# Two graph-attention layers in one timetable: further shifts for the places of the steps

## Chip, cores, metric

The kernel runs on one core of a Trainium2 chip. The metric is the device time of one execution in microseconds. The time before is the median of three runs; one further execution was profiled.

## What is computed

Sixteen graphs of 1024 nodes with 256 features pass through two pre-normed layers that share one adjacency matrix. The first layer holds an MLP, an attention without a mask (call it Dense), a second MLP and a masked attention (`a`); the second layer is one masked attention (`b`). Cut to what matters:

```python
def reference(x, adj, w1, b1, w2, b2, W_fc, a_fc, W_hand, a_hand, W_l1, a_l1):
    h = maximum(layernorm(x), 0)
    res = relu(h @ w1 + b1)
    out = elu(gat(res, None, W_fc, a_fc, slope=0.2)) + res      # Dense: every node sees all
    res = relu(out @ w2 + b2)
    x = x + relu(elu(gat(res, adj, W_hand, a_hand, slope=0.2)) + res)   # a
    h = maximum(layernorm(x), 0)
    return x + relu(gat(h, adj, W_l1, a_l1, slope=0.01))                # b
def gat(inp, mask, W, a):
    h = inp @ W
    e = leaky_relu((h @ a[:F])[:, :, None] + (h @ a[F:])[:, None, :])
    return softmax(where(mask, e, -inf), axis=2) @ h            # elu after it inside the first layer
```

## The kernel before

Each graph is one "batch" `b` of eight row tiles of 128 nodes. The softmax weights factor: for `a` and `b` a weight is the larger of two products of a node's number with a neighbour's, times the 0/1 mask. So VectorE makes a tile of weights in one instruction (`weight`, L645: tiles `atta` and `attb`, 128 x 256) from a row that is broadcast over the partitions (`rows`), and TensorE multiplies two such tiles of 128 with a tile of projected features (`product`, L655). A column of numbers becomes a broadcast row by way of DRAM: TensorE turns it (`send_row`, L474), ScalarE copies the 8 x 128 line (L476) and issues its DMA to `row_a`, `row_b` or `row_r` (L477); SyncE, after the line has landed, issues the read that broadcasts it (`row`, L630 for `a` and `b`, L759 for Dense). In the last batches TensorE broadcasts the row itself.

Dense has no mask, so from the second batch on it is not a product of matrices: nodes are ranked (`rank`, VectorE, L786 to L793), scattered in order of rank to DRAM (`scatter`, GpSimd indirect DMA, L800, one for each tile of nodes; it needs that tile's `project(t, 0)`, its `fs` copy at L744 and its rank), read back sorted (`read_sorted`, SyncE, L844, tile `xs`), summed from both ends (`sum_before`, `sum_behind`, tiles `tt` and `xs`), written as tables (`write_table`, L879; `carry`, L896 and L901) and gathered (`gather`, GpSimd, L912: a fine and a coarse one for each tile). `share` and `mean` make the mean, `merge` (L984 to L988) and `merge_end` (L994, and GpSimd's add at L995) turn and add it, `mlp2` (L1002, copy by ScalarE L1005) follows. `Norm` takes statistics (`stats`, L494, `root`, L499 and L500), centers (`center`, L504) and turns tiles on TensorE (`turn`, L514, copy L518); `BlockNorm` moves blocks by DMA instead (`move`, L560). `natural` turns the second MLP's output back (L1016, L1018).

Every one of 6508 steps stands in a list with a time that was written by hand, and a shift is added to it:

```python
    def at(name, lo, hi, steps):
        for i, step in enumerate(steps):
            key = part + name
            moved = SHIFT.get(key, ())
            k = turn[key] = turn.get(key, -1) + 1
            when = lo + (hi - lo) * i / len(steps) + (moved[k] if k < len(moved) else 0.0)
            table.append((when, len(table), step))
```

`part` is "start " ahead of the first period, then "first ", "mid " (batches 1 to 12) and "end " (the last three); `turn` counts the uses of a name inside one period. A missing entry is a shift of nothing. At the end the list is sorted by `when`, and the steps are emitted in that order. On TensorE, VectorE, ScalarE and SyncE the instructions run in that order exactly, and the scheduler is told to keep GpSimd's order too, the scatters free among themselves. Times in the list do nothing but sort: no instruction waits for a clock. A step that stands in a queue waits for its operands and holds up all that stands behind it.

A period is 142 of the list's units for each batch: `masked_first` (attention `a`), `second_norm`, `masked_second` (products of `b`, the last three quarters of them in the next batch's period), `dense_sums`, `early_gathers`, `dense_end` for the next batch and `first_mlp`, `dense_rows`, `dense_begin` for the one after it. In `masked_first` the order of `a` is `masked_first1` (`vectors`: the three exponentials of the factors), `masked_first2` (`send`), `masked_first3` (`row`), `weights a` and `masked_first9` (`product`). PSUM has four buffers named `mm` for products and projections; ScalarE or VectorE must have read one before it is used again. Tiles of weights have eight buffers, broadcast rows two.

Of the kernel before, what the change touches and what calls it, by code (L numbers as in the profile page):

```python
# [30 lines left out]
    "end dense_begin5": (3.85, 3.85,),  # L31
    "end dense_begin6": (0, 0, 0, -3.04, -3.77, -12.93,),
    "end dense_begin7": (5.89,),
    "end dense_end1": (-6.28, -0.87,),
    "end dense_end2": (1.33, -1.87, -0.43, -1.02, 1.01, 1.01, 1.01, 1.01,),
    "end dense_rows1": (-5.54, 0, 0, -5.65, 0, 0, -5.89, -12.08,),
    "end dense_sums10": (-30.04,),
    "end dense_sums12": (6.2,),
    "end dense_sums2": (7.2, 0, 16.96, 0, -1.45, 0, 4.23, 7.81,),
    "end dense_sums3": (-5.9, -5.22,),  # L40
    "end dense_sums4": (-1.96, -1.96, -1.96, -1.96,),
    "end dense_sums6": (5.6,),
    "end dense_sums7": (0, -0.43, -1.68, -1.93, -2.8, -4.51, 0, 2.83,),
    "end dense_sums9": (4.27,),
    "end early_gathers1": (2.05, 8.49,),
    "end early_gathers2": (2.39, 2.39,),
    "end early_gathers3": (0, 0, 0, 13.54,),
    "end early_gathers4": (3.94, 3.94, 3.94, 3.94, 3.94, 3.94, 3.94, 3.94,),
    "end first_mlp1": (-4.68, 0, 0, 5.61,),
    "end first_mlp2": (0, 0, 0, -3.18,),  # L50
    "end masked_first1": (-5.71,),
    "end masked_first10": (0, -1.8, -2.88, -3.79, -1.77, 1.09, -1.61, -2.39,),
    "end masked_first11": (0, 0, 1.72, 0, -1.95, 0, -1.34, -1.8,),
    "end masked_first12": (-2.14, -0.57,),
    "end masked_first13": (1.32, 1.3, 0.19, -1.57, -1.22, 0, -0.9, -0.54,),
    "end masked_first14": (1.17, 2.08, 1.51, 0, 5.36, 0, 2.26,),
    "end masked_first16": (1.34,),
    "end masked_first2": (-5.62,),
    "end masked_first4": (-2.61,),
    "end masked_first5": (-3.63, -2.25, -1.64, -1.44,),  # L60
    "end masked_first7": (-16.12, -7.04, 0, 27.99,),
    "end masked_first8": (-14.41, 0, 0, -12.41,),
    "end masked_first9": (-1.61, -1.61, -1.61, -1.61, -1.61, -1.61, -1.61, -1.61, -3.83, -3.83,
        -3.83, -3.83, -3.83, -3.83, -3.83, -3.83, -1.88, -1.88, -1.88, -1.88, -1.88, -1.88, -1.88,
        -1.88, -4.28, -3.4, -3, -2.75, -2.49, -2.68, -1.93, -2.03, -6.69, -6.37, -6.2, -4.96,
        -5.03, -3.23, -2.35, -1.84,),
    "end masked_second1": (0.66, 0.66, 0.66, 0.66, 0.66, 0.66, -2.34, -2.03, -0.87, -1.67, 0, 0,
        -3.2, -3.01, -2.28, -2.11, -1.88, -1.38, 0, 0, 0, 0, 0, 0, -4.13, -2.16, -1.71, -1.96, 0,
        1.01, -5.79, -3.22, -2.37, 0, 0, 3.34,),
    "end masked_second2": (0, 0, 0, 0, -1.59, 0.14, 1.34, 1.34, 2.34, 1.98, 0, 3.96,),  # L70
    "end masked_second3": (0, -1.37, 1.51, 0, 0, 2.39, 1.49, 3.1,),
    "end masked_second4": (2.68, 5.78, 3.49, 0, 1.55, 1.12, 1.78, 5.03,),
    "end masked_second5": (12.24, 5.75, 8.78, 18.18, 17.51, 10.76,),
    "end masked_second6": (7.07, 9.36,),
    "end merges1": (0, -1.03, -0.3, -2.41, 4.74, 0.64, 1.64,),
    "end merges2": (-0.27, -1.56, -1.28, 3.77, 3.14,),
    "end scatters1": (4.29, -1.28, 0, -3.35, 0, -3.76, 0, -5.98,),
    "end second_mlp1": (1.75, 3.03, 13.57,),
    "end second_mlp2": (-7.98, -7.98, -7.98, -7.98, -7.98, -7.98, -7.98, -7.98,),
    "end second_mlp3": (-6.19,),  # L80
    "end second_norm1": (-2.07, 0, -0.95, -3.91, -2.7, -3.39, -4.37, -5.24,),
    "end second_norm2": (-5.55,),
    "end second_norm3": (-5.42,),
    "end second_norm4": (-3.38,),
    "end second_norm5": (-3.12, -0.71, -6.35, -2.61, -0.69,),
    "end second_norm6": (-1.66,),
    "end turn_at1": (0.72, 5.74, 4.57, 6.67, 0.93, 0.93, 0.93, 0.93,),
    "end turn_at2": (2.47, 2.47, 2.47, 2.47, 0.67, 0.87, 0.71, 0.9,),
    "end weights a": (-4.01, -4.48, -2.31, 0, -2.36, 0, 0, 2.96, -5.53, -0.61, -1.24, 0, -8.38,
        -6.95, 0, 0.62, -1.94, 0, -4.51, -7.54, -1.94, 0, 0, 0, -3.5, -22.43, -2.3, -2.55, -4.46,  # L90
        -0.67, -3.44, -19, -5.33, -5.1, -4.83, -26.42, -2.06, 0, -5.18, -4.76,),
    "end weights b": (-2.94, -1.93, 0, -4.78, -1.01, -0.6, 0, 2.13, -2.64, 0.84, -5.47, 0, 0.22,
        -2.95, -0.53, 1.64, -4.25, -7.92, -4.22, -2.6, -2.98, -9.67, -4.08, 0.95, 1.1, 0, 0, 0,
        -5.56, -0.87, 0, 1.83, -4.94, -2.59, -2.4, -4.98, 0, 2.22, 3.49, 2.79, -2.87, -2.87, -2.87,
        -2.87, -2.87, -2.87, -2.87, -2.87,),
    "first dense_begin2": (1, 4.41,),
    "first dense_begin3": (-1.89,),
    "first dense_begin4": (0, -3.14,),
    "first dense_begin5": (-13.99, -4.89,),
    "first dense_begin6": (-10.16, -24.55, -16.26, -13.59, -20.39, -20.4,),  # L100
    "first dense_begin7": (26.94,),
    "first dense_begin8": (8.17,),
    "first dense_end1": (0, -4.85,),
    "first dense_rows1": (0, 14.27, -1.34, 0, 0, 0, 0, -10.26,),
    "first first_mlp1": (0, 4.41, 24.43,),
    "first first_mlp2": (5.97, 17.04, 15.82,),
    "first first_norm3": (-21.29, -20.06, -15.24, -17.2, -23.42, -19.12, -5.58, -19.77,),
    "first first_norm4": (-1.34,),
    "first first_norm5": (0, -2.84, 6.7, -8.53,),
    "first first_norm6": (16.39, 14.37, 17.56, 0, 0, 8.81, 12.12, 10.28,),  # L110
    "first first_norm7": (27.8, 27.8, 27.8, 27.8,),
    "first first_norm8": (21.34, 21.34, 21.34, 21.34,),
    "first gathers1": (0, 0, 0, 0, 10.07, 13.53, 11.92, 8.19,),
    "first gathers2": (1.94, 0, 0, 7.94, 0, 0, 0, -4.73,),
    "first masked_first1": (-3.19,),
    "first masked_first10": (0, 0, 0, -0.95, 0, 0, -0.98,),
    "first masked_first11": (3.59, 0, 2.07, 0, 3.1, 0, -2.17, 0.49,),
    "first masked_first13": (0, 4.59, 0, 0, 3.21, 0, -3.57, -3.16,),
    "first masked_first14": (2.35, 8.59, 1.68, 0, 2.92, 1.37, -3.45, -4.07,),
    "first masked_first15": (-2.27,),  # L120
    "first masked_first16": (-4.48,),
    "first masked_first4": (-3.2,),
    "first masked_first9": (0, 0, 0, 0, 0, 0, 0, 0, 0, 0, 0, 0, 0, 0, 0, 0, -1.65, -1.65, -1.65,
        -1.65, -1.65, -1.65, -1.65, -1.65,),
    "first masked_second1": (-6.69, -6.69, -6.69, -6.69, -6.69, -6.69, -5.31, -5.31, -5.31, -5.31,
        -5.31, -5.31,),
    "first masked_second2": (-5.39, -5.39, -3.53, -3.53,),
    "first masked_second3": (-5.97, 0, 0, 0, 0, 0, 4.48,),
    "first masked_second4": (7.23, 7.93, 0, 0, 20.56, 0, 15.38,),
    "first masked_second6": (44.24, 33.84,),  # L130
    "first merges1": (0, -0.51, 0, 3.1, 0, 0.67, 0, 1.56,),
    "first merges2": (1.94, 1.94, 1.94, 1.94,),
    "first scatters1": (0, 0, 0, 0, 0, 0, 11.81, 7.33,),
    "first second_mlp1": (0, 0, 7.25,),
    "first second_mlp2": (-6.32, -6.32, -6.32, -6.32, -6.32, -6.32, -6.32, -6.32,),
    "first second_norm1": (1.12, 0.5, 4.9, 2.6, 5.13, 3.86, 3.83, 2.75,),
    "first second_norm2": (2.35,),
    "first second_norm7": (-3.9,),
    "first second_norm8": (10.06, 8.39, 6.47, 15.18,),
    "first start51": (-5.5,),  # L140
    "first turn_at1": (-7.72, -9.85, -6.6, -9.06,),
    "first turn_at2": (-8.2, -6.53, -6.35, -4.27,),
    "first weights a": (0, 0, 0, 0, 0, 0, 0, 0, 0, 0, 0, 0, 0, 0, 0, 0, 0, 0, 0, 0, 0, 1.81, 2.27,
        0, 0, -3.96, -13.89, -7.05, -4.57,),
    "first weights b": (-10.9, -6.04, -9.42, -13.57, -24.74, -13.19, -25.26, -13.17, -9.33, -2.06,
        -2.02, -10.77, -3.64, 0, 0, -19.37, -3.07, -1.96, -1.75, -3.62, -5, -4.1, -5.96, 0, -15.31,
        0, 0, 0, 0, -18.05,),
    "mid dense_begin1": (-4.18,),
    "mid dense_begin3": (-5.24,),
    "mid dense_begin5": (-10.75,),  # L150
    "mid dense_begin6": (0, 0, -21.24, -17.26, -3.32, -3.92,),
# [1683 lines left out]
```

## Time and profile before

| | us |
| --- | --- |
| median of three runs (lowest, highest) | 2287.52 (2285.39, 2288.34) |
| the profiled execution, its own time | 2288.26 |
| its span, first to last instruction | 2286.5 |
| TensorE busy | 2217.3 (97%) |
| VectorE busy | 1626.2 (71%) |
| ScalarE busy | 1263.9 (55%) |
| GpSimd busy | 958.8 (42%) |
| granted TensorE clock | 0.997 |

Busy time is summed for each engine over the span; 1.8 us of the execution lie outside it. A row of a group of instructions gives the line, the engine, out<-in with shapes and count, then busy us and mean ns of one, then the idle time just before them and who ended it. A row of waits gives who waited, for whom, the us in total, the number of times and the longest. A row of the timeline gives start and length in us, the instruction, and in brackets the idle time before it.

### The profile page before, as it was taken

Reading aid. Unit: us, or ns where it says so; the run is one execution under the profiler, and the core shown is the slowest. Engines: PE = TensorE matmul, PEld = TensorE weight load, DVE = VectorE, ACT = ScalarE, POOL = GpSimd, SP = SyncE. Lnnn points to the kernel's source line nnn. Section 1 sums busy time; section 2 is a strip of 40 time slices with the busy share of each in tenths; the row PEclk is TensorE's granted clock in tenths of the full one; section 3 lists DMA queues with packets and bytes.
Section 4 is the critical chain, followed back from the end, with each engine's and each line's share of the span. In section 5 each row is a group of like instructions: output and inputs, shape, how many; then the busy total and the mean of one; then the engine's idle time right before and its main releaser. Section 6 shows DMA issues by size and latency. Waiting matters only on the chain. (4 is left out here: it accounts for less than half of the span.)

```text
span 2286.5 us, 31026 instructions
## 1 busy us (share of the span) xinstructions
PE 2217.3 (97%) x9754; PEld 1721.6 (75%) x9754; DVE 1626.2 (71%) x4535; ACT 1263.9 (55%) x2797; POOL 958.8 (42%) x1212
## 2 busy tenths in 40 slices
PE   8989999999999999999999999999999999999997
PEld 5766677787877868777787877868777787878776
DVE  7667586676867768776676867768776776858755
ACT  5355656557465563746557374564755557365552
POOL 1253325263442635436263442636435263443520
PEclk9999999999999999999999999999999999999999
DMA  4568367574666747567674666747466674655600
GB/s 175 179 175 199 87 183 181 163 204 126 204 134 186 191 145 201 122 188 171 178 191 133 196 134 188 191 149 205 117 202 152 184 194 133 179 117 170 180 21 28
DMA packets 263870, 368.95 MB, mean 161 GB/s; under 512 B 124353, under 2 KB 175881, under 8 KB 259601
## 3 DMA queue, kind: packets, MB, share of 16 engines
q1 hardware_dynamic: 217088, 202.72, 32.0%
q0 software_dynamic: 45952, 163.99, 27.6%
q8 instruction: 80, 1.31, 0.2%
q14 instruction: 94, 0.76, 0.1%
q10 hardware_dynamic: 656, 0.17, 0.0%
HBM read 226.88 MB, written 126.29 MB: 154 GB/s over the span
## 5 line engine op out<-in xcount | busy, mean ns | idle before, releaser
L655 PE MATMUL oa<-hma,atta 128*128 128x258 f32 x2048 | 463.9, 383 | 20.8 <-DVE atta L645 18.2
L655 PE MATMUL ob<-hmb,attb 128*128 128x257 f32 x2048 | 467.0, 381 | 4.1 <-DVE attb L645 4.1
L740 PE MATMUL h<-wfc_sb,resT 128*128 128x257 f32 x2048 | 468.1, 379 | 0.0
L655 PEld LDWEIGHTS oa<-hma,atta 128*128 128x128 f32 x2048 | 383.6, 190 | 90.1 <-issue 27.0
L655 PEld LDWEIGHTS ob<-hmb,attb 128*128 128x128 f32 x2048 | 383.4, 190 | 72.5 <-issue 13.3
L740 PEld LDWEIGHTS h<-wfc_sb,resT 128*128 128x128 f32 x2048 | 379.7, 189 | 71.5 <-issue 19.7
L683 POOL TENSOR_TENSOR posa<-posa,onat 128x256 f32<-128x256 f32 x118 | 107.6, 912 | 485.7 <-ACT posa L671 485.6
L645 DVE SCALAR_TENSOR_TENSOR attb<-rowsb,qwdb,edge 128x256 f32<-128x256 f32 (+1 forms) x536 | 256.3, 497 | 51.6 <-PE ob L655 38.1
L645 DVE SCALAR_TENSOR_TENSOR atta<-rowsa,qwda,edge 128x256 f32<-128x256 f32 (+1 forms) x520 | 249.7, 513 | 58.2 <-DMA rowsa<-row_a 50.5
L995 POOL TENSOR_TENSOR resT<-resT,e 128x512 f32<-128x512 f32 x128 | 164.0, 1283 | 270.5 <-DVE e L994 245.7
L912 POOL DMA_INDIRECT got<-coarse,k x124 | 204.1, 1646 | 112.7 <-DMA got<-fine,k 73.1
L726 PE MATMUL m<-hT,w_sb 128*128 128x512 f32 x512 | 237.5, 598 | 0.6 <-ACT hT L518 0.5
L1002 PE MATMUL m<-resT,w_sb 128*128 128x512 f32 x512 | 230.9, 595 | 2.9 <-POOL resT L995 2.6
L697 ACT ACTIVATE rb<-ob,recb 128x256 f32<-128x256 f32 x128 | 59.0, 474 | 314.5 <-DVE recb L695 302.7
L670 ACT ACTIVATE ea<-oa,reca 128x256 f32<-128x256 f32 x128 | 60.6, 473 | 240.5 <-DVE reca L667 224.1
L912 POOL DMA_INDIRECT got<-fine,k x124 | 129.4, 1043 | 102.8 <-DVE attd L958 38.3
L1002 PEld LDWEIGHTS m<-resT,w_sb 128*128 128x128 f32 x512 | 94.8, 191 | 100.2 <-issue 87.1
L726 PEld LDWEIGHTS m<-hT,w_sb 128*128 128x128 f32 x512 | 94.3, 192 | 86.4 <-issue 77.9
L800 POOL DMA_INDIRECT sorted<-hnat,place x128 | 129.5, 1011 | 41.7 <-issue 23.9
L823 ACT ACTIVATE junk<-r,fs 128x1024 int8<-128x1024 f32 x124 | 142.2, 1147 | 6.4 <-ACT linea L476 4.5
L986 DVE TENSOR_SCALAR e<-hpT 128x512 f32<-128x512 f32 x128 | 86.4, 679 | 80.9 <-PE hpT L984 65.3
L994 DVE SCALAR_TENSOR_TENSOR e<-hpT,e 128x512 f32<-128x512 f32 x128 | 87.9, 687 | 47.7 <-ACT e L988 47.2
(195 smaller groups left out, 3420.7 us busy)
## 6 DMA issues: line engine op xcount, KB each, us to landing
xs<-sorted SPq DMA_DIRECT2D x32, 1028.0 KB
fine<-tt SPq DMA_DIRECT2D x32, 1026.0 KB
fine<-xs SPq DMA_DIRECT2D x32, 1026.0 KB
x<-in_x_dram SPq DMA_DIRECT2D x16, 1024.0 KB
xn<-in_x_dram SPq DMA_DIRECT2D x15, 1024.0 KB
out_dram<-x SPq DMA_DIRECT2D x28, 512.0 KB
hT<-xn SPq DMA_DIRECT2D x416, 32.0 KB
coarse<-carry SPq DMA_DIRECT2D x32, 256.5 KB
```

The lines of the kernel that those rows point to most:

```text
L645: nc.vector.scalar_tensor_tensor(a_t[:, :n * P], self.rows[:, i], self.qwd[:, 1, j:j + 1], edge[:, j, i], op0=OP.max, op1=OP.mult)
L655: nc.tensor.matmul(self.out[t][:, :F + self.ONES], lhsT=self.att[t0, j][:, (t - t0) * P:(t - t0 + 1) * P], rhs=self.hm[:, j, 2:2 + F + sel ...
L683: adder.tensor_add(pos, pos, o_nat[:, t, :])
L726: nc.tensor.matmul(ps, lhsT=w1_sb[:, kc, c * P:(c + 1) * P], rhs=piece(kc, h), start=(kc == 0), stop=(kc == FC - 1))
L740: nc.tensor.matmul(ps[:, :F + 1], lhsT=self.resT[:, kc, t * P:(t + 1) * P], rhs=wfc_sb[:, kc, g, :], start=(kc == 0), stop=(kc == HC - 1))
L800: made = nc.gpsimd.indirect_dma_start(out=sorted_d[self.b % 2], out_offset=bass.IndirectOffsetOnAxis(ap=self.place[:, t:t + 1], axis=0), i ...
L823: nc.scalar.activation(junk, self.r2, AF.Sign, bias=self.fs[:, 0, t:t + 1], accum_out=self.signs[:, t:t + 1])
L912: nc.gpsimd.indirect_dma_start(out=got[u // n][:, u % n, :], out_offset=None, in_=(coarse_d if coarse else fine_d)[self.b % 2][:, :], in_o ...
L986: nc.vector.tensor_scalar_min(e, ps, 0.0)
L994: nc.vector.scalar_tensor_tensor(e, ps, 0.0, e, op0=OP.max, op1=OP.add)
L995: nc.gpsimd.tensor_add(dst, dst, e)
L1002: nc.tensor.matmul(ps, lhsT=w2_sb[:, kc, c * P:(c + 1) * P], rhs=self.resT[:, kc, h * HALF:(h + 1) * HALF], start=(kc == 0), stop=(kc == H ...
```

## The change

The table `SHIFT` is replaced: 197 keys before, 215 after, nearly all values differ. No other line of the program changes, and no instruction is added, removed or resized. The values came from a search over a model of the program in which the lines of the rows, and the reads of them, land later than in the model behind the old values. Cut to the entries that the prediction speaks of (many keys hold one value per step):

```diff
-    "mid masked_first1": (2.17,),
-    "mid masked_first2": (1.67,),
+    "mid masked_first2": (-2.08,),
-    "mid weights a": (-0.95, -1.77, -0.69, -0.29, -1.4, -6.11, 0, 0, -4.55, -7.3, 0, 0, 0, 0, 0, 0,
+    "mid weights a": (-5.61, -5.61, -5.61, -5.61, -5.61, -5.61, -5.61, -5.61, -3.71, -9.93, -3.34,
...
+    "mid dense_begin4": (2.24, 0, -1.8, 0, -9.71,),
-    "mid dense_begin6": (0, 0, -21.24, -17.26, -3.32, -3.92,),
+    "mid dense_begin6": (-11.19, 0, -28.74, -20.88, -19.69, -15.58,),
+    "mid dense_begin7": (-8.63,),
+    "mid dense_sums1": (-47.98,),
-    "mid scatters1": (-1.68, -1.68, -1.68, -1.68, -1.68, -1.68, -1.68, -1.68,),
+    "mid scatters1": (0, 0, -7.81, 0, -16.13,),
-    "mid second_norm9": (12.89,),
+    "mid second_norm9": (-12.33,),
-    "mid masked_second1": (-6.06, -4.38, -4.96, -4.4, -4.02, -4.85, -2.93, -3.71, -0.98, -1.47,
+    "mid masked_second1": (-19.72, -6.34, -5.21, -5.4, -5.04, -4.23, 0, 0, 0, 0, 0, 0, 0, 0, 0, 0,
...
-    "mid masked_second3": (0, 0, 1.76, -0.96, 3.75,),
+    "mid masked_second3": (-1.99, -2.6, 0.2, -1.04, 0, 0, 0, 24.02,),
-    "mid turn_at1": (0, 0, 2.19, -5.82,),
-    "mid turn_at2": (3.05, 3.05, 3.05, 3.05, 4.51, 4.51, 4.51, 4.51,),
+    "mid turn_at1": (2.3, 2.3, 2.3, 2.3, 3.13, 3.13, 3.13, 3.13,),
+    "mid turn_at2": (0, 0, 0, 3.05, 4.36, 4.36, 4.36, 4.36,),
-    "start start27": (11.76, 5.71,),
+    "start start27": (-2.71,),
-    "start gathers2": (8.37, 12.36, 13.46, 9.14,),
+    "start gathers2": (0, 7.74, 0, 4.99,),
```

For batch 5, whose period starts at 682 in the list, this puts `vectors` at 683.00 (685.17 before), `send` at 683.32 (687.07), the first product of `a` at 697.55 (700.00), `project(t, 0)` of the Dense of batch 6 for t = 2, 6 and 7 at 649.81, 649.98 and 656.25 (661.00, 666.35 and 667.91) and its scatters in the order 4, 2, 0, 1, 3, 5, 6, 7 (0 to 7 before).

## The prediction

> **What bounds the kernel now.** I read the page's first part, then TensorE's waits by stage, then the timeline of one period.
>
> ```profile
> span 2286.5 us, 31026 instructions
> PE 2217.3 (97%) x9754; PEld 1721.6 (75%) x9754; DVE 1626.2 (71%) x4535; ACT 1263.9 (55%) x2797; POOL 958.8 (42%) x1212
> ```
>
> TensorE is the bound. Of its 69.2 us without work, 10.8 lie before its first transpose and about 10.6 after its last one (ended near 2275.9); no place in a timetable removes the 2217.3. So all that this change can win is in some 48 us of gaps. Where they are, by TensorE's waits, first in 250 to 1900 us (twelve alike periods of 137 us), then in 0 to 250 us:
>
> ```profile
> PE oa L655 <- DVE atta L645: 17.4, 12, 1.9
> PE pa L592 <- issue: 0.8, 1, 0.8
> ```
>
> ```profile
> PE nt L514 <- DVE hn L504: 14.3, 3, 10.8
> PE hpT L984 <- issue: 4.0, 1, 4.0
> PE m L1002 <- POOL resT L995: 2.6, 2, 2.1
> ```
>
> The middle has one fault, 1.45 us in every period; the start has 10.8 (the first load) and some 15 more; the end (1900 on) has 12 us in pieces of up to 1.2. The fault, by the timeline of the period of batch 5:
>
> ```profile
> 841.33 0.80 SPq L844 DMA_DIRECT2D xs<-sorted  x2
> ...
> 844.66 0.27 ACTq L477 DMA_DIRECT2D row_a<-linea  x1
> ...
> 849.76 0.32 SPq L630 DMA_DIRECT2D rowsa<-row_a  x1
> ...
> 854.19 0.48 DVE L645 SCALAR_TENSOR_TENSOR atta<-rowsa,qwda,edge 128x256 f32<-128x256 f32 x1 [4.58 <-DMA rowsa<-row_a]
> ```
>
> The line of 4 KB is issued at 844.66, and SP gets past its landing 5.1 us later; the read of the rows takes 4.4 more; VectorE has stood 4.58 us. Then TensorE waits for the third atta, since before computes j = 5, 1, 0 in that order and product j = 0 comes first: it starts at 856.28. The same kind of line without big company:
>
> ```profile
> 811.64 0.27 ACTq L477 DMA_DIRECT2D row_r<-line  x1
> ...
> 812.86 0.34 SPq L759 DMA_DIRECT2D r<-row_r  x1
> ```
>
> 1.2 us. So the line of `a` is late because 2 MB of xs, issued 3.3 us ahead of it, are in its way; and xs is issued at 841.33 because of the last scatter:
>
> ```profile
> 828.67 1.11 POOL L800 DMA_INDIRECT sorted<-hnat,place  x1 [0.30 <-issue]
> 832.06 0.19 POOL L744 COPY fs<-hnat 128x1 f32<-128x1 f32 x1 [2.29 <-ACT hnat L742]
> ...
> 838.45 0.97 POOL L800 DMA_INDIRECT sorted<-hnat,place  x1 [0.30 <-issue]
> 841.32 0.53 POOL L859 MEMSET tt<- 128x513 f32 x1 [1.91 <-DMA sorted<-hnat,place]
> ```
>
> GpSimd stood 2.29 us for a projection and then issued scatters back to back every 1.3 us up to 838.45, though the last rank was ready at 834.9.
>
> **What the Trainium skill says.** *DMA: Bandwidth & Descriptors*, "Queues, rings and completion order": SP and ACT own one ring each on the same 16 engines, and an engine drains a whole packet of one ring before it turns to another. The trace agrees: 5.1 us behind xs, 1.2 alone. The same page, "Anatomy of one DMA", puts some 2 us of fixed cost on a DMA, most of it the write's receipt; here the lone line took 1.2, and I use that. *TensorE: Matmul & The Clock Gate*, "Step-by-step": only weight loads are pulled ahead, matmuls stay in order; so a late atta stops all of TensorE, as the 17.4 us show.
>
> **The change, part by part.** A step's time is lo + (hi - lo) i / n + shift; sorting all 6508 steps by it gives each queue's order, before and after. No instruction is added or taken away; what counts is how much of TensorE's work lies between two steps. I price it from back-to-back rows: 28 passes of 258 columns in 6.26 us are 0.22 a pass, 0.87 for a masked product of two tiles or a projection of `a` or `b`, 1.74 for a `project` of Dense or an `mlp1`.
>
> *Rows of `a`, twelve periods.* (i) Scatters: `project(t,0)` for t = 6, 7, 2 move 16.4, 11.7 and 11.2 us earlier in the timetable, rank 4 comes first, and the scatters go 4, 2, 0, 1, 3, 5, 6, 7. None waits then for a projection, and GpSimd (1.3 us a scatter) keeps up with VectorE (about 2 us a rank). The memset of tt, which stood in the queue behind the scatters, goes 48 us earlier. Between the first rank and rank 7 stand 1.3 us of other VectorE work (two weights, `query`), as much as the weight and its wait in before, and the row r is read no later (SP's four moves ahead of it, 16 issues of 0.65 us, fit before its line lands). So rank 7 is ready near 834.5, its scatter goes out at once, and xs is issued near 834.5 + 2.9 = 837.4 (838.45 to 841.33 in before), 4 us earlier. (ii) `vectors` to first product holds 12.1 us of TensorE work after and 13.4 before. On the clock of this period `vectors` begins at 841.4 (841.04 in before, and 0.4 more of TensorE's work is ahead of it); the line is issued 3.3 later, 844.7; the last of xs lands near 837.4 + 7.5 = 844.9; the line by 846.2; rows 4.4 later, 850.6; the first atta, now j = 0, at 851.1. TensorE comes there at 841.4 + 12.1 = 853.5: 2.4 us to spare. If xs does not move, rows land at 854.1, atta at 854.7, and 1.2 of the wait stay. I take the first and leave 0.9 us over twelve periods: **-16.5** (ends -3 and -17.4).
>
> *Waits that come in their place, twelve periods.* `center` 4 to 7 of the second norm now stand behind `finish(6)` of `b` on VectorE. From the end of its product: 0.45 drain, 0.16 reciprocal, four centers at 0.4, `update(6)` between them held by ScalarE's 0.47: the last is ready at 2.8; TensorE has 1.74 (two projections) and three turns of 0.22 before it needs it, 2.4: some 0.4 us. `vectors` of `a` waits for the last projection's copy, behind sign 6 (1.26 us) on ScalarE: 0.15 to 0.2. The copy of `mlp2(1,1)` now stands behind `query`, just on time. Sum 0.6 a period: **+7** (ends 0 and +14). Behind a center that waits there are only centers on VectorE, and the turn and projections on TensorE.
>
> *Start.* `carry` 0 and 1 move 16.6 and 7.9 us of TensorE work earlier, so the coarse gathers (issued 121.91 to 134.25 in before) can go from about 115, and the merges that stood 4.0 + 0.7 us at 144 find their data. The second norm of batch 0 turns some 9 us of TensorE work later, which covers its 3.5. Against it: four allocations of a PSUM buffer with 0 to 0.87 us of work since its last use, where a copy takes 0.9 to 1.4: +2. The 2.6 at 156 stays. Of -6 I take **-4** (ends -8 and +2).
>
> *End.* In batch 14 `vectors` to first product of `b` grows from 3.0 to 5.6 us of work, against 4.8 that it took; in 15 by 0.4 for `a` and `b`. -3 is in sight, but this stretch changes most and I follow it least: **-1.5** (ends -5 and +4).
>
> Other moves (stores, loads of x, the reads of rows `b` 25 us earlier, atts up to 20 us ahead) I cost at nothing: the least work between a weight and its product grows from 0.9 to 2.6 us for `a` and from 1.7 to 4.4 for `b`, and TensorE's work covers them. Without that cover each late weight is 0.5 us. SP's queue: gb's read no longer stands before a move that it could hold up, and the load of x, now ahead of the first table write, delays that by up to 5 us, which has 28 us until its gather.
>
> Sum -16.5 + 7 - 4 - 1.5 = -15. The profiled execution took 2288.26 (span 2286.5 and 1.8 around it), which gives 2273.3; it lies 0.7 over the median of the runs, 2287.52, from which I predict **2272.5**.
>
> **Rivals.** *The line stays behind xs* (r, ranks or scatters no faster; or the plan's order is not the bound of GpSimd): the rows' part gives only the atta order, -3 to -5, new waits +3 to +7, start and end -5: 2282 to 2288, no difference. For it: 1 us of delay in r's row shifts the whole chain. Against: 2.4 us of slack.
>
> *Slower: PSUM buffers held too long.* The first product of `b`, (0,2,0), moves 13.7 us earlier, ahead of the two mlp1, and holds two of the four `mm` buffers until its finish; `finish(7)` moves 24 us later and holds one. At seven places a period only 1.74 us of work is left between a buffer's last use and its next (2.62 in before). The copy needs 0.9, with one sign ahead of it on ScalarE 2.2, which is 0.45 of stall. At four places a period that is 1.8 us, twelve times: +22, with -17.4 + 7 - 5.5: 2294. It decides from about 1.9 us of new waits a period on. Against: ScalarE is 55% busy, and by my count most copies come 0.1 to 0.5 us before they are needed.
>
> That the change does nothing is excluded: the order differs on every queue.
>
> **Numbers.** Gain as worked out 0.72 (own range 2262 to 2282); no difference 0.14; buffers or another new wait 0.14. The range 2261 to 2291 leaves out the far ends. About 0.2% (4.6 us) is what a measurement of this kernel can tell from no change.
>
> **What would show it.** Right: the atta wait of oa falls under 3 us, xs is issued about 4 us earlier against `vectors`, the line takes under 2 us, the 4.0 at 144 is gone; `nt <- hn` of about 5 us appears. Wrong: `m`, `h`, `pb` or `ob` waits on ScalarE's copies over 1.5 us a period, or atta still near 15.

## The result, and the profile after

| | before | after |
| --- | --- | --- |
| median of the runs, us | 2287.93 (2285.39 to 2288.96, 4 runs) | 2250.35 (2248.43 to 2251.37, 4 runs) |
| ratio, with its 95% interval | | 0.9836 (0.9819 to 0.9853) |
| span of the profiled execution | 2286.5 | 2249.6 |
| TensorE without work ahead of its first, between, and after its last matmul | 10.8, 47.8, 10.6 | 11.1, 21.0, 10.3 |

37.6 us were gained where 15 were forecast, and the time lies 11 us below the range. From the changed kernel's page, the lines that answer to the first two of the prediction:

```profile
span 2249.6 us, 31025 instructions
PE 2207.2 (98%) x9754; PEld 1723.4 (77%) x9754; DVE 1643.1 (73%) x4535; ACT 1259.6 (56%) x2797; POOL 954.4 (42%) x1212
```

The two counts of instructions differ in semaphore waits alone. The span is 36.9 us shorter, and only 26.8 of that is idle time of TensorE: its **busy time fell by 10.1**, with the same 9754 matmuls. TensorE's waits in 250 to 1900 us (who <- for whom, us in total, times, longest):

```profile
PE m L748 <- ACT rb L719: 1.1, 2, 0.8
PE oa L677 <- DVE atta L667: 0.9, 2, 0.7
PE hpT L1006 <- DVE hp L959: 0.5, 2, 0.3
```

The 17.4 us of waits for atta are 0.9, and no other row of over 1.1 us has come. The same view of 0 to 250 us:

```profile
PE nt L536 <- POOL rstd L522: 11.1, 1, 11.1
PE hpT L1006 <- DVE got L959: 1.4, 2, 0.9
PE m L1024 <- POOL resT L1017: 1.0, 2, 0.8
```

The first load is as long as it was; the 4.0 at the merges is gone, the 2.6 behind GpSimd is 1.0, and of `nt <- hn` 0.3 is left in the first 250 us.

**An account that does not depend on idle rows.** I take, for each of TensorE's 9754 matmuls, the time to the next one's start, less the median of that time for its kind over the two traces. What is over is time that issue lost, be it shown as idle or not. The medians add up to 2189.1 us in every kernel here, as the matmuls are the same; the rest is loss. (From either trace alone the medians add up to 2189.1 and 2189.2, so the matmuls themselves are no faster after the change.)

| loss by starts (idle part), us | 0 to 250 | 250 to 1900 | from 1900 | sum |
| --- | --- | --- | --- | --- |
| before | 23.1 (14.6) | 34.1 (21.1) | 18.5 (12.2) | 75.7 |
| after | 13.4 (5.8) | 9.5 (3.9) | 15.9 (11.3) | 38.8 |
| change | -9.7 | -24.6 | -2.6 | -36.9 |

That the last column gives the 36.9 us of the span follows from the definition. What the account adds is where the loss was, and that part of it counts as busy: the part that isn't idle is 27.9 us before and 17.8 after, and the difference is the 10.1. In batch 5 of before the starts are late by 2.05, 0.07, 0.23, 0.08, 0.23, 0.10 and 0.10 us: 2.9 us, where the view of waits put down 1.9.

The chain of the row of `a` in the changed kernel, by the timeline of one period (its `vectors` start near 825):

```profile
819.38 0.97 POOL L822 DMA_INDIRECT sorted<-hnat,place  x1 [1.94 <-DVE place L815]
```

```profile
822.26 0.81 SPq L866 DMA_DIRECT2D xs<-sorted  x2
...
828.49 0.27 ACTq L499 DMA_DIRECT2D row_a<-linea  x1
830.10 0.32 SPq L652 DMA_DIRECT2D rowsa<-row_a  x1
...
834.54 1.28 DVE L667 SCALAR_TENSOR_TENSOR atta<-rowsa,qwda,edge 128x256 f32<-128x256 f32 x3 [2.55 <-DMA rowsa<-row_a]
...
837.48 1.25 PE L677 MATMUL oa<-hma,atta 128*128 128x258 f32 x5
```

The last scatter no longer waits in a row of others but for its own rank. xs is issued 6.2 us ahead of the line (3.3 in before), the line lands in 1.6 (5.1), the first atta starts 6.1 after the line's issue (9.5), and TensorE comes to it 9.0 after: it has been ready for 2.5 us. In eleven of the twelve periods the first product starts without a wait. In the first, xs is only 1.8 us ahead of the line, the line takes 4.7, and 0.7 us of the wait stay.

### The profile page after: what moved, and what is told of

It is laid out like the page before. It is cut to its first block, busy times and chain, and to the rows that moved or that the text cites. A ratio compares the mean times of both kernels' runs of the same rounds, so it can differ in the third digit from the quotient of the medians.

```text
span 2249.6 us, 31025 instructions
## 1 busy us (share of the span) xinstructions
PE 2207.2 (98%) x9754; PEld 1723.4 (77%) x9754; DVE 1643.1 (73%) x4535; ACT 1259.6 (56%) x2797; POOL 954.4 (42%) x1212
## 4 chain that ended last, share of the span: by engine, by line
PE 75%; DVE 6%; DMA 2%; POOL 2%; ACT 1%; issue 1%; POOLq 0%; DVEq 0%; ACTq 0%; SPq 0%
PE oa L677 17%; PE h L762 16%; PE ob L677 14%; PE m L1024 8%; PE m L748 6%; PE pa L614 4%; PE pb L614 3%; PE hpT L1006 2%; DMA got<-coarse,k 2%; DVE attb L667 1%; PE carry L918 1%; PE on L1038 1%; PE nt L536 1%; DVE stats L516 1%; DVE hp L959 1%
## 5 line engine op out<-in xcount | busy, mean ns | idle before, releaser
L762 PE MATMUL h<-wfc_sb,resT 128*128 128x257 f32 x2048 | 462.8, 379 | 0.0
L667 DVE SCALAR_TENSOR_TENSOR attb<-rowsb,qwdb,edge 128x256 f32<-128x256 f32 (+1 forms) x536 | 292.1, 563 | 34.6 <-PE ob L677 28.6
L667 DVE SCALAR_TENSOR_TENSOR atta<-rowsa,qwda,edge 128x256 f32<-128x256 f32 (+1 forms) x520 | 257.3, 524 | 51.4 <-DMA rowsa<-row_a 35.6
L764 ACT COPY hnat<-h 128x257 f32<-128x257 f32 x256 | 90.8, 367 | 104.1 <-PE h L762 101.6
```

The costliest lines, as they stand in the source:

```text
L667: nc.vector.scalar_tensor_tensor(a_t[:, :n * P], self.rows[:, i], self.qwd[:, 1, j:j + 1], edge[:, j, i], op0=OP.max, op1=OP.mult)
L762: nc.tensor.matmul(ps[:, :F + 1], lhsT=self.resT[:, kc, t * P:(t + 1) * P], rhs=wfc_sb[:, kc, g, :], start=(kc == 0), stop=(kc == HC - 1))
L764: nc.scalar.copy(self.h_nat[:, t, g, :], ps[:, :F + 1])
```

## The experiments

All but three are built from the two tables alone: a kernel takes some lists from the changed table and the rest from before's. The three (a_scatters_cover, a_order_finish, a_both_mended) have one to six numbers changed by hand, which are shown. The instructions are the same everywhere and only their order differs. Ratios are to before on the same chip.

**First four: parts of the change alone.** I went in with a theory D (stalls are longer than their idle rows, and nearly all of the middle's hang on the row of `a`), against the prediction's own sums (W).

*The scatters alone* (label a_scatters):

```diff
+    "mid dense_begin4": (2.24, 0, -1.8, 0, -9.71,),
-    "mid dense_begin6": (0, 0, -21.24, -17.26, -3.32, -3.92,),
+    "mid dense_begin6": (-11.19, 0, -28.74, -20.88, -19.69, -15.58,),
+    "mid dense_sums1": (-47.98,),
-    "mid scatters1": (-1.68, -1.68, -1.68, -1.68, -1.68, -1.68, -1.68, -1.68,),
+    "mid scatters1": (0, 0, -7.81, 0, -16.13,),
```

> Of the change only four lists of the middle part: the scatters, the projections and ranks ahead of them, and the memset of tt; the order of the atts and products stays that of before (5, 1, 0). Theory D (a stall of TensorE is longer than its idle row shows, because the drain of the matmul ahead of it counts as busy): by the starts of its matmuls before loses 34.0 us in 250 to 1900 us, of which only some 21 are idle; almost all of it hangs on the late rows of a. If xs goes out some 3 us earlier against the line, the line takes under 2.5 us, atta j = 0 as third is ready near 7.5 us after the line's issue and TensorE comes near 9.6: the stall is gone, the time is 2288 - 24 = 2264 (2260 to 2268), and the busy time of TensorE falls by 6 or more. Theory W (only the idle rows can be won, as the prediction had it; what fell of the busy time in the changed kernel comes from elsewhere in the table): -17, 2271, busy time unchanged at 2217. If the scatters are not what held xs: 2285 to 2288.

Measured: 1.0005 (0.9995 to 1.0014), no gain at all. Yet the chain did what it should: in nine of the twelve periods xs is issued 5.5 to 6.0 us ahead of the line, the read follows the line in 1.7 to 2.3, and the first product starts 9.57 us after it without a wait (11.6 in batch 5 of before). In two others xs is 5.9 and 5.3 us ahead and the read still comes 3.4 and 3.7 us after the line, so the distance to xs isn't all of it. The waits of TensorE in its middle:

```profile
PE extdps L446 <- DVE e L971: 15.8, 11, 1.4
PE oa L632 <- DVE atta L622: 1.7, 3, 0.8
```

The stall has changed its place. The timeline of TensorE shows where:

```profile
803.18 3.60 PE L979 MATMUL m<-resT,w_sb 128*128 128x512 f32 x8
806.61 0.60 PE L961 MATMUL hpT<-ident,hp 128*128 128x128 f32 x4
807.05 0.27 PE L451 MATMUL line_ps<-ident,fs 128*8 128x128 f32 x1
808.76 0.29 PE L446 MATMUL extdps<-ident,extd 128*128 128x128 f32 x1 [1.43 <-DVE e L971]
```

The transpose of `highest` follows the merge directly, and waits until `merge_end` on VectorE has read the merge's PSUM. In before `project(4, 0)`, 1.74 us of TensorE work, stood between:

```profile
808.82 1.90 PE L740 MATMUL h<-wfc_sb,resT 128*128 128x257 f32 x8
...
810.67 0.27 PE L469 MATMUL extdps<-ident,extd 128*128 128x128 f32 x1
```

The new place of that projection, which lets its scatter go early, took the cover away. In the whole change eight matmuls of `mlp2` stand there instead (3.60 us from 790.82), and nothing waits.

*The order of atts and products alone* (a_order): `mid weights a` and `mid masked_first9` from the changed table, nothing else.

> Of the change only two lists of the middle part: the places of the atts of a (weights a) and of the products of its first half (masked_first9). The scatters stay late, so the line still goes behind xs, 4.3 to 5.2 us. Theory D and theory W differ only in size: atta j = 0 is computed first and not third, so the product can start about 1 us earlier, at the cost that later atts may be late in their turn. D: 12 periods of 1.0 to 1.5 us, 2270 to 2276. W: -3 to -5 as in the prediction's first rival, 2283 to 2285.

Measured: 1.0205 (1.0187 to 1.0223), **47 us slower**, where both theories had it faster. The wait for the first atta is gone, as expected. But this row has come into its middle:

```profile
PE oa L630 <- ACT rb L672: 46.8, 12, 4.9
```

and VectorE's timeline in one of those waits (TensorE stands until 880.15):

```profile
867.48 1.28 DVE L620 SCALAR_TENSOR_TENSOR atta<-rowsa,qwda,edge 128x256 f32<-128x256 f32 x3 [5.28 <-DMA rowsa<-row_a]
...
877.52 1.53 DVE L862 SCALAR_TENSOR_TENSOR xs<-xs,bd 128x513 f32<-128x513 f32 x2
878.97 0.48 DVE L620 SCALAR_TENSOR_TENSOR atta<-rowsa,qwda,edge 128x256 f32<-128x256 f32 x1
879.37 0.22 DVE L670 RECIPROCAL recb<-ob 128x1 f32<-128x1 f32 x2
```

The products of `b` that this reciprocal divides by were through near 868.6. But `finish` stands behind fifteen atts and the sums of Dense, and these stood behind the row: VectorE waited 5.28 us for it. The product of `a` that needs the PSUM buffer of `finish` waits 4.62 us. My prediction had a rival with held PSUM buffers, at 1.8 us a period; here is its mechanism, through VectorE's queue and not through ScalarE's copies, at over twice the price. By starts the middle loses 78.5 us, 44 more than in before: 48.8 in this wait, and 21.7 after it, while TensorE's granted clock stands at one half (see the last section).

*Both together* (a_both):

> The six lists of the two kernels before together, nothing else of the change. Theory D: the same loss is taken away that the scatters alone take, so no sum of the two: 2262 to 2266, idle for atta under 2 us in the middle, TensorE's busy time 2210 or less. Theory W: 2271, busy time 2217. Were the two parts independent, their gains would add up.

Measured: 1.0198 (1.0181 to 1.0215). Theory D fell for these parts, as W did: neither a sum nor a shared gain, but both new waits side by side (oa behind rb 31.0 us by starts, extdps 17.6), with 15.1 us at half the clock on top.

*The start alone* (start_first): the 102 lists with start and first.

> Of the change only the lists whose names begin with start and first (ahead of batch 0 and batch 0 itself), 102 of them; middle and end as before. By TensorE's starts the first 250 us lose 23.2 us before and 13.4 in the changed kernel. Theory D: -10, 2278 (2276 to 2280). The prediction's term for the start was -4: 2284. A rival: the start's gain needs the middle's order too (the turn from batch 0 to batch 1 lies in both), then under 4 us.

Measured: 1.0012 (1.0005 to 1.0019). The first 250 us lose 15.0 and not 23.1, as the account said; but the middle loses 43.6 and not 34.1, most of it where the new batch 0 meets the old batch 1: 14.8 us from 250 to 524, where before loses 6.1. (Of the 43.6, 5.0 are at half the clock, after waits of 1.9 to 2.7 us.) The gain is there and is given back at the seam.

**Theory C** was formed on these: a place is good only together with the steps that cover it or queue behind it; a part of the change alone trades one wait for another. Four kernels to test it.

*One number more to the scatters* (a_scatters_cover):

```diff
-    "mid dense_begin6": (-11.19, 0, -28.74, -20.88, -19.69, -15.58,),
+    "mid dense_begin6": (-11.19, 0, -21.24, -20.88, -19.69, -15.58,),
```

> The kernel with the scatters alone (a_scatters), with one number of the table more: project(4, 0), which it had taken from between the merges and highest, is left where before has it. a_scatters took its place of the 19.3 us of atta waits 17.6 us at the transposes extdps of highest (1.6 in eleven of twelve periods), which stand one 1.74 us projection closer behind the merges and wait for the PSUM buffer that merge_end gives back. Theory C (a part of the change only trades one wait for another as long as the steps that cover it don't move with it): with the projection back the 1.6 go, no other wait takes their place, mid loss falls from 28.6 to about 11, 2266 on the chip of the first four runs (before 2284 there): 0.992 of before. Theory L (that stretch of TensorE is bound by something else, such as the e chain on ScalarE and VectorE, and the wait only shows elsewhere): 2280 to 2284 again.

Measured: **0.9903** (0.9887 to 0.9919), some 22 us faster than before. Its middle:

```profile
PE oa L632 <- DVE atta L622: 2.6, 3, 1.1
PE pa L569 <- ACT hma L571: 0.8, 1, 0.8
```

The extdps row is gone and nothing took its place; loss in the middle is 12.5 us (a_scatters 30.5, where the expectation wrote 28.6; before 34.1, the whole change 9.5). So four lists of the middle, with one number of before, do 21.6 of the middle's 24.6 us. How much each of the four does was not tried. The busy time of TensorE is 2212.1, 5.2 less than before.

*Five numbers more to the order* (a_order_finish):

```diff
-    "mid masked_second3": (0, 0, 1.76, -0.96, 3.75,),
+    "mid masked_second3": (-3.9, -4.45, 1.76, -0.96, 3.75,),
-    "mid dense_sums4": (-0.8, -1.89, -1.48, -2.25, -1.88, -1.88, -1.88, -1.88,),
+    "mid dense_sums4": (-0.8, -1.89, -1.48, -2.25, -1.88, 1.0, 0, 0,),
```

> The kernel with the order of atts and products alone (a_order), with five numbers of the table more: finish(0) and finish(1) of b go up to their products' end on VectorE (shift -3.9 and -4.45) and sum_before 5, 6, 7 go behind them. In a_order the atts of a, moved up, stand ahead of the finishes: a product of a waited 4.78 us for the PSUM buffer that finish gives back (oa <- ACT rb 48.8 us over the middle). Moved up, the finish has 5.1 us less VectorE work ahead of it. Theory C: the wait goes, and with it the small ones behind it; the first product still starts without idle time although the line is as late as in before, because atta 0 comes first: 0.992 of before (2266). If the finish must wait for its own product on VectorE and so holds the atts up: 1.000 or slower.

Measured: 1.005 (1.0036 to 1.0063): 35 us better than a_order, and still behind before. The waits of its middle:

```profile
PE oa L630 <- DVE atta L620: 13.0, 11, 1.2
PE oa L630 <- ACT hma L614: 8.4, 11, 1.3
PE oa L630 <- ACT posa L646: 3.1, 13, 0.6
PE oa L630 <- ACT rb L672: 2.0, 1, 2.0
```

The wait for the buffer is gone as forecast (46.8 to 2.0), so its cause is shown. The forecast of the time missed: later products now wait for a later atta, for a scaled tile of features and for ScalarE. In the whole change these waits are not there, so the new order needs more of the table than I mended; which entries was not tried.

*Both, mended* (a_both_mended): the six lists of a_both with the six numbers.

> The six lists of a_both with both mends (project(4, 0) left as cover; finishes up, sum_before 5 to 7 behind them). Theory C: once no wait of a is left, the second remedy adds nothing: 0.991 to 0.993 of before, within 0.2% of the better of the two others. If the two remedies take away different losses, it is faster than either by 5 us or more.

Measured: 0.9997 (0.9989 to 1.0005), a miss. With the rows in time, the order of atts still costs the 18 us that a_scatters_cover has not: loss in the middle is 30.5 us, 17.5 of it in `oa` behind atta and posa. Of the change's two remedies for the row of `a`, the earlier scatters are the one that pays; the order pays nothing in this company.

*Taken out of the whole change* (after_finish_back): `mid masked_second3`, `mid masked_second4` and `mid dense_sums4` as in before.

> The changed kernel with three lists of the middle put back to before's: the finishes and updates of b (masked_second3, masked_second4) and the sums (dense_sums4). Theory C: the buffer wait of a_order (oa <- ACT rb) comes back, 3 to 4.6 us a period less what the earlier rows give: 1.000 to 1.008 of before, where the changed kernel has 0.984, a loss of 38 to 55 us for steps that I priced at nothing. If these steps have slack in the changed kernel: 0.984 to 0.987.

Measured: 0.9948 (0.9935 to 0.9961), 26 us worse than the whole change: less than the 38 to 55 I wrote, and more than the other forecast (0.984 to 0.987) allows.

```profile
PE oa L648 <- ACT rb L690: 13.0, 22, 2.0
```

The same wait as in a_order, twice in nearly every period and shorter; by starts it is 16.6 of the 21.7 us that the middle loses more. Steps that I had costed at nothing are worth 26 us in this company: they keep the new order of atts from costing. Whether they gain anything without that order was not tried.

**The stages, two at a time.**

*Middle and batch 0* (mid_and_first, 115 lists):

> The lists of the middle and of batch 0 (names with mid and first, 115 of them) as changed; those ahead of batch 0 and of the last three batches as before. By TensorE's starts, before loses 75.7 us in all after its first matmul and the changed kernel 38.8. Theory C with the accounts of the stages: the middle's 24.7 are kept, batch 0 keeps the changed kernel's 8.7 in 100 to 250 us (before 20.0), the end stays at before's 18.5: loss near 41, ratio 0.984 to 0.986. If the start's own lists are needed for batch 0 (as start_first lost 8.7 us in 250 to 524 where its lists met before's middle): loss 45 to 55, ratio 0.987 to 0.991.

Measured: 0.9871 (0.9854 to 0.9888); loss 42.3 us, 16.7, 6.5 and 19.1 by stage. The loss is near the first forecast's 41, the ratio just inside the second's range; it does not decide between them. Batch 0's gain comes with the middle; from 0 to 250 us before's start keeps 3.3 us more than the whole change (the merge's 5.2 at 145 us stay).

*All but the end* (without_end, 62 lists put back):

> The changed kernel with the lists of the last three batches (62 names with end) put back to before's. The end's term by the starts of TensorE's matmuls: 18.5 us lost from 1900 on in before, 15.9 in the changed kernel. Theory C: +2.6 us on the changed kernel's 0.9836 of before: 0.984 to 0.986. The prediction's term was -1.5. If before's end meets the changed middle badly, as start_first did: 0.988 or more.

Measured: 0.9861 (0.9845 to 0.9878); loss 40.6 us, of it 18.5 from 1900 us on, as in before. The end's term is -2.6 by the account. The ratio is 0.0025 over the whole change's, with intervals that overlap, so the times neither confirm nor correct that.

No mixture beat the whole change.

## Why the prediction was wrong, step by step

The account has -36.9 where the prediction's sum is -15. Of the 21.9 us between, the rows of `a` have 8.8, the new waits 6.3, the start 5.7 and the end 1.1.

- **"All that this change can win is in some 48 us of gaps."** This is the step that failed first: I took TensorE's busy time for work that no order can remove, and priced each wait by its idle row. The work is 2189.1 by starts, not 2217.3; the loss between starts was 75.7, of which the 48 are the idle part. The gain stayed under 48; what missed was not the ceiling itself but the price of each wait. A stall of one matmul is longer than its idle row, as the row starts only when the profile ends the matmul ahead: 1.434 us idle are 1.598 by starts in a_scatters, 4.620 are 4.783 in a_order, 0.16 each time. The Trainium skill, *TensorE: Matmul & The Clock Gate*, "Single matmul latency", gives 166 ns as the part of the latency that isn't streaming, for a single bf16 matmul at full clock. The 0.16 is of that size, but these are fp32 matmuls and their ends are modelled in the profile, so it says how the rows are drawn and is no measurement of a drain. A wait under 0.16 shows no idle row at all. In the middle of before, some 6.8 of the 13 us of loss that isn't idle are these 0.16 on 42 stalls with an idle row, and 6.1 are late starts without any.
- **Rows of `a`, -16.5.** The chain went as forecast: xs 3 us earlier against the line (4 forecast), the line 1.6 (1.5), the atta at 6.1 after the line's issue (6.4), TensorE there at 9.0 (8.8), 0.9 us of idle left (0.9). The term was mis-sized by the point above: by starts the products of `a` lost 26.9 us in the middle of before and 1.6 after, **-25**, and 7.5 of it had not been idle. One part of the forecast chain was not needed: a_scatters_cover gets nearly all of this gain in the old order of atts and products.
- **New waits, +7.** They are not there: the other losses of the middle went from 7.2 to 7.9. Of the signs that the prediction named for being right, only this one, about 5 us of `nt <- hn`, did not come. For `center` 4 to 7 I added up whole durations from the end of the product. Here is VectorE in a middle period, and TensorE below it:

```profile
757.38 0.17 DVE L717 RECIPROCAL recb<-ob 128x1 f32<-128x1 f32 x1 [1.18 <-PE ob L677]
757.47 0.72 DVE L526 TENSOR_SCALAR hn<-x,mv,rstd 128x256 f32<-128x256 f32 x2
758.15 0.42 DVE L723 TENSOR_TENSOR x<-x,rb 128x256 f32<-128x256 f32 x1
758.49 0.73 DVE L526 TENSOR_SCALAR hn<-x,mv,rstd 128x256 f32<-128x256 f32 x2
```

```profile
757.62 1.91 PE L614 MATMUL pb<-wl_sb,hT 128*128 128x258 f32 x8
759.36 1.03 PE L536 MATMUL nt<-ident,hn 128*128 128x128 f32 x8
```

  The reciprocal starts 0.24 us before the stretch of products gives way to projections (the other tile of the pair ends last); instructions on VectorE follow each other every 0.31 to 0.37 us, not every 0.40; and the update between them finds ScalarE's result there. The last center is through at 759.22, 1.6 us after the projections began and not 2.8; TensorE needs it at 760.0. A wait of 0.4 was forecast, and 0.8 us of slack is there.
- **Start, -4.** -9.7. By starts, in us: the merges' gathers 5.0 to 2.7 (I had said 4.7 of idle go); `nt <- hn` 3.8 to 0.6, as forecast; `m <- resT` behind GpSimd 3.0 to 1.3, where I had said that it stays; the 1.9 of `hpT <- e` at 244, which lay in the start's 15 us and which I had not priced, are gone. Of the +2 for PSUM buffers nothing stands out; new are 0.7 at extdps and 1.2 at `nt <- hT`. That is -7.2 in all. There is one more term, which I had not seen: in before TensorE's granted clock fell to one half for 3.4 us after the wait at 144, and for 3.4 more after the waits of 1.3 and 2.2 us that end at 218.5, 3.2 us of late starts together; the changed kernel has no such stretch in 100 to 250 us. The wrong steps are the two waits that I had left standing and this term, put at nothing.
- **End, -1.5.** -2.6 by the account; which moves gave it was not followed.
- **"Other moves I cost at nothing."** Alone they were not tried. But without their company the parts that I priced would have brought 0 (a_scatters) or +47 us (a_order); putting three lists back costs 26. The move of `project(4, 0)`, 7.5 units, is not among the three that the prediction lists, and its old place was the cover that a_scatters lost. A sum of independent parts was the wrong form for it.
- **The rivals.** The line didn't stay behind xs. Held PSUM buffers are real, as a_order shows, but the whole change moves the finishes along; with the finishes put back (after_finish_back) the wait returns.

## What to carry to other kernels

Measure what a bound engine loses from start to start, not from its idle rows: 1.45 us a period of idle was 2.2 us of loss here, and a fall of "busy" time can be stalls that went. When a step is moved, ask what its old place covered: 1.74 us of one projection, left in place, made the difference between no gain and 22 us. And price a reordering as a whole; a part of it that is tried alone may only move the wait to the next instruction in the queue.

## What was not expected of the hardware

After some pauses TensorE ran at half its clock for 3.4 or 6.8 us. In the view by stretches a line has the stretch and its length, the busy time and count of TensorE's matmuls and weight loads, VectorE, ScalarE and GpSimd, then the granted clock, and DMA's share and GB/s. The first line is from before, after the waits of 1.3 and 2.2 us; the second from a_order, after a wait of 4.62:

```profile
219.70:223.10 3.40, 3.40 (x5) 1.35 (x4) 2.82 (x10) 2.69 (x6) 2.58 (x4) 0.50 0.93 234
```

```profile
879.95:883.30 3.35, 3.15 (x7) 2.52 (x8) 1.55 (x6) 0.51 (x2) 0.00 (x0) 0.50 1.03 177
```

In a_order all eleven waits of 3.6 to 4.9 us in the middle had such a stretch, which began between 1.8 us ahead of the wait's end and 0.9 us after it. In it 7 to 15 matmuls were late by 0.21 us each for 258 columns, 1.5 to 3.0 us on top of each wait. In a_both six of nine waits of 2.42 us had it and three did not. One wait of 1.86 us in start_first and one of 1.60 in after_finish_back were followed by it within a microsecond; before's waits of up to 1.90 us in the middle never were. So in these runs the length of a wait alone does not tell whether the clock falls. The mean granted clock of a_order is 0.986, before's 0.997. The Trainium skill, *TensorE: Matmul & The Clock Gate*, "HAM oscillation — how this bites in real kernels", warns of pauses over some 3.4 us; here 2.42 and less were enough at times, and the measurement decides.
